# A slot of its own for each expert's first 128 pairs, listed and gathered earlier, in a two-layer mixture-of-experts kernel

## The chip, the cores and the metric

The kernel runs on one core of a Trainium2 chip. The metric is the device time of one execution, in microseconds (us). A core has a matrix engine, TensorE (PE, with its weight loads shown as PEld), and VectorE (DVE), ScalarE (ACT) and GpSimd (POOL). Each takes its instructions in the order of its own queue. SyncE (SP) only issues DMAs; ACT and POOL issue some too. The program's order of instructions on each engine is fixed when the kernel is built; at run time they wait for one another through semaphores.

## The reference

The input is 2048 tokens (8 batches of 256) of 512 numbers. Two layers follow, each a token mixing step and a mixture of eight experts of which every token uses two; each adds its result to the residual `x`:

```python
x = x + _L0_ffn_ref(_L0_cond_ref(x, ...), ...)   # paged windowed attention, then experts
x = x + _L1_ffn_ref(_L1_cond_ref(x, ...), ...)   # linear with a low-rank adapter per batch, then experts

# layer 0 experts: a common W plus a sparse change per expert
logits = jnp.clip(xt @ gate_w.T, -50.0, 50.0)
top_w, top_idx = jax.lax.top_k(logits, TOP_K)
rw = jax.nn.softmax(top_w, axis=-1)
...
# layer 1 tokens: H + (x A_b^T) B_b^T s_b, with the adapter b chosen for each batch
# layer 1 experts: top 2 of a softmax, two linear layers with biases and a gelu
h = jnp.einsum('th,ehi->eti', x, fc1_w) + fc1_b[:, None, :]
h = jax.nn.gelu(h, approximate=False)
y = jnp.einsum('eti,eih->eth', h, fc2_w) + fc2_b[:, None, :]
out = jnp.einsum('eth,te->th', y, combine)
```

## The kernel before

All is float32. Tokens are 16 tiles of 128 rows. The kernel has these stages, in program order:

1. Preparation: rotary tables, old and new keys and values, and `delta_d`, the experts' weight matrices of layer 0, made in DRAM.
2. Attention (`attend`, `gate_rows`), a loop over eight batches `b` with two tiles each. Each `attend` does four head pairs: scores `ps` (PE), mask and maximum (DVE), exponential (ACT), scaling by the sum (DVE), transposes `pp` (PE), copies `pT` (ACT) and products `po` with the values, which are copied into `oT`. `gate_rows` computes the two tiles' expert logits `lg0` with `pg` and `pt`. The PSUM pool `ps_o` has two buffers, tag "misc", for `po`, `pk`, `pq`, `pt`, `pg` and `ph`. A generator `beside` is stepped within `attend`: in the batches 6 and 7 it copies `delta_0`, half of the experts' matrices, into place (L623, ACT). `output_rows` (`ph`, L635) makes rows of `h_d`, the attention's result, for tiles 0 to 8 during the loop.
3. Middle stage of layer 0. `routing_constants`, `top2` and `normalized` choose two experts and their coefficients for all 16 tiles. `route` ranks the (token, expert) pairs of each expert and gives each pair a slot and a row. `fill_slots` turns this into lists: for each slot its 128 tokens (`token_i`) and their coefficients (`weight`), by 32 accumulated PE products `pm` of one-hot matrices `hot` (the row) and `put` (the slot). The rows 9 to 15 of `output_rows` run beside it, and the second half of the matrices, `delta_1`, is copied on POOL and ACT. Then `fold_adapters` loads layer 1's adapters and transposes and scales them (PE: `pw`, `pgb`, `pbg`).
4. The expert slots of layer 0 (`slots0`). There are 34 slots of 128 rows: a full slot belongs to one expert that is known when the program is built, a paired slot to two experts with 64 rows each, the second of which is found at run time (`owners`). `Plan` says how many of each there are: 8 full and 26 paired. A slot gathers its rows with an indirect DMA issued by POOL (`fetched`, L533, three slots ahead), turns them (`pa`, L569), multiplies by the expert's matrix (`py`, L547 full, L556 paired), scales (ACT) and adds to `sums_d` by an indirect DMA (`added`, L580). SP loads layer 1's weights `w1` and half of `w2` as soon as their memory is free. `run_rest` is a conditional part (L1752) for pairs that found no place.
5. Tokens of layer 1. The gate is folded with the adapters (`fold_gate`); the sums are read back, transposed and multiplied by the low-rank parts (`inner`), then by `wc` (`outer`). Both go over four quads of four tiles. `outer` writes `g_d` by DMAs issued from ACT. The routing of layer 1 is the same `route`, on DVE beside `outer`.
6. The expert slots of layer 1 (`slots1`): 22 full and 12 paired, gathered from `g_d`, with two matrices each (`pu` L1978, `py`), and added to `out`.

`token_i` has values up to 2175: rows from 2048 up are the filling of unused places. `h_d` and `g_d` have 128 additional rows for them, set to zero by two DMAs. The gathers of a slot in stage 4 read `h_d` as a whole, and those of stage 6 `g_d` as a whole, so each waits for every write of that tensor.

Of the kernel before, what the change touches and what calls it, by code (L numbers as in the profile page):

```python
# [19 lines left out]
P = 128  # L20
# [32 lines left out]
class Plan:  # L53
# [5 lines left out]

    PAIRED, FULL = 128 * HR, 256 * HR  # L60

    def __init__(self, full, side):
        self.full = [e for e in range(E) for _ in range(full[e])]
        self.side = [e for e in range(E) for _ in range(side[e])]
        self.F, self.D = len(self.full), len(self.side)
        self.n = self.F + self.D
        self.by_expert = []
        for e in range(E):
            t = HR * side[e]
            u = t + P * full[e]  # L70
            second = self.PAIRED + HR * (self.F + sum(side[:e]))
            whole = self.FULL + P * sum(full[:e]) - t
            first = HR * self.F - u
            self.by_expert.append((t, u, second + 1, whole - second, first - whole))


PLAN0 = Plan([1] * E, [3] * 6 + [4] * 2)
PLAN1 = Plan([3] * 6 + [2] * 2, [1] * 6 + [3] * 2)
# [3 lines left out]
def two_layer_kernel(ctx: ExitStack, tc: tile.TileContext, io: dict, out: bass.AP):  # L82
# [9 lines left out]
    h_d = dram.tile([N + P, D], F32, name="h_d")  # L92


    g_d = dram.tile([N + P, D], F32, name="g_d")
# [47 lines left out]
    def routing_constants(pool, plan=None, late=False):  # L143
# [36 lines left out]
        nc.gpsimd.iota(tok_i, pattern=[[P, NT]], base=-N, channel_multiplier=1)  # L180
# [7 lines left out]
        if plan:  # L188
            fixed_i = pool.tile([P, 5, E], I32, name="fixed_i")
# [14 lines left out]
            fixed = pool.tile([P, 5, E], F32, name="fixed")  # L204
# [5 lines left out]
    def ranks(pool, psum, consts, sel):  # L210

        earlier, ahead, same_e = consts[:3]
        flat_sel = sel.rearrange("p i e -> p (i e)")
        pst = psum.tile([P, P], F32, name="pst", tag="route_a")
        nc.tensor.transpose(pst, flat_sel, ident)
        tot = pool.tile([P, 1], F32, name="tot")
        nc.vector.tensor_reduce(tot, pst, AX.X, ALU.add)
        pn = psum.tile([P, E], F32, name="pn", tag="route_a")
        nc.tensor.matmul(pn, tot.to_broadcast([P, P]), same_e, start=True, stop=True)
        prk = psum.tile([P, NT, E], F32, name="prk", tag="route_b")  # L220
        prk2 = prk.rearrange("p i e -> p (i e)")
        nc.tensor.matmul(prk2, earlier, flat_sel, start=True, stop=False)
        nc.tensor.matmul(prk2, tot.to_broadcast([P, P]), ahead, start=False, stop=True)
# [22 lines left out]
    def two_rows(pool, rows, cf, row, coef):  # L246
# [4 lines left out]
        at = pool.tile([P, NT, E], F32, name="at")  # L251
        nc.vector.tensor_tensor(
            at, row, rows[:, 1, :, None].to_broadcast([P, NT, E]), ALU.is_equal
# [20 lines left out]
    def fill_slots(keep, pool, psum, tag, consts, slot, rem, cf, n, at_once):  # L274
# [3 lines left out]
        what = pool.tile([P, 2, NT], F32, name="what")  # L278
        nc.vector.tensor_tensor(
            what,  # L280
            tok[:, None, :].to_broadcast([P, 2, NT]),
# [5 lines left out]
        pm = psum.tile([P, 2, n], F32, name="pm", tag="route_b")  # L287
        STEP = 4
        for j in range(0, 2 * NT, STEP):
            if j % at_once == 0:  # L290
                span = slice(j, j + at_once)
                put = pool.tile([P, at_once, 2, n], F32, name="put", tag="wide")
# [18 lines left out]
            hot = pool.tile([P, STEP, P], F32, name="hot", bufs=2)  # L311
# [6 lines left out]
            for k in range(STEP):  # L318
                nc.tensor.matmul(
                    pm.rearrange("p c s -> p (c s)"),  # L320
                    hot[:, k, :],
                    put[:, (j + k) % at_once].rearrange("p c s -> p (c s)"),
                    start=(j + k == 0),
                    stop=(j + k == 2 * NT - 1),
                )
        token_i = keep.tile([P, n], I32, name=f"token_i_{tag}")
# [244 lines left out]
    def turned(pool, psum, xs):  # L571
# [3 lines left out]
        nc.vector.tensor_copy(xsT, pa)  # L575
        return xsT

    def added(sum_d, token_i, s, y):

        nc.gpsimd.indirect_dma_start(  # L580
            out=sum_d,
# [1546 lines left out]
```

## Time and profile before

| | us |
|---|---|
| median of three runs | 968.81 |
| the three runs | 976.61, 968.81, 968.16 |
| profiled execution | 970.09 |
| its span | 968.4 |
| mean granted TensorE clock, share of full speed | 0.979 |

Where the stages lie in the span of the profiled execution, by the first and last instruction of each in the trace:

| stage | from | to |
|---|---|---|
| last value product of the attention | | 397.6 |
| output rows 9 to 15 | 400.4 | 426.8 |
| list products and adapters | 426.8 | 437.6 |
| slots of layer 0 | 442.3 | 585.7 |
| tokens of layer 1 | 587.0 | 684.1 |
| slots of layer 1 | 695.3 | end |

The page counts how long each engine executed instructions; time in which it waits for a semaphore is idle. PEld runs beside PE. In a line of the timeline the first number is the start within the span, the second the duration, and in square brackets stands the idle time of that engine before it, with what released it. A row of the list of waits gives total time, number and longest of the waits of one kind. Line numbers (L533) are those of the kernel before.

### The profile page before, as it was taken

How to read it: one execution, taken by the hardware profiler on the slowest of the kernel's cores; microseconds unless marked ns; L12 is line 12 of the kernel's file. 1: busy time of each engine (PE TensorE's matmuls, PEld its weight loads, DVE VectorE, ACT ScalarE, POOL GpSimd, SP SyncE). 2: the span in 40 equal slices, each digit the busy share in tenths (PEclk: the TensorE clock that was granted, in tenths of full speed). 3: DMA queues.
4: the chain of work that ended last, by engine and by line, in shares of the span. 5: the costliest groups of instructions: out<-in, count | busy, mean ns of one | idle time of the engine just before them, and what ended most of it. 6: DMA issues, size and time to landing. Idle time of an engine off the chain costs nothing. (4 is left out here: it accounts for less than half of the span.)

```text
span 968.4 us, 14307 instructions
## 1 busy us (share of the span) xinstructions
PE 901.9 (93%) x4829; PEld 491.8 (51%) x4829; DVE 455.5 (47%) x1487; ACT 371.8 (38%) x954; POOL 360.3 (37%) x335
## 2 busy tenths in 40 slices
PE   6998889999999997897999997999599999999995
PEld 3554445655555554464433333545377777753332
DVE  5788898846857766672211112470022223223332
ACT  3676475736647599631111113401111111122221
POOL 2721656557564200405666641000233333333211
PEclk9899999999999999997999999999799999999998
DMA  6587692342432212529997768961524443443322
GB/s 194 215 307 269 225 322 45 98 114 60 138 78 61 61 44 66 189 85 326 341 255 133 129 89 222 364 230 54 185 55 76 73 69 66 77 69 63 50 27 34
DMA packets 74237, 134.62 MB, mean 139 GB/s; under 512 B 17309, under 2 KB 22941, under 8 KB 74032
## 3 DMA queue, kind: packets, MB, share of 16 engines
q0 software_dynamic: 25088, 43.68, 24.2%
q1 hardware_dynamic: 38496, 74.57, 22.1%
q10 hardware_dynamic: 10576, 15.39, 4.3%
q8 instruction: 41, 0.67, 0.3%
q14 instruction: 36, 0.29, 0.1%
HBM read 89.95 MB, written 52.56 MB: 147 GB/s over the span
## 5 line engine op out<-in xcount | busy, mean ns | idle before, releaser
L533 POOL DMA_INDIRECT xs<-g_d,token_i_l x34 | 35.2, 1035 | 230.1 <-PE pa L569 129.5
L575 DVE COPY xsT<-pa 128x512 f32<-128x512 f32 x68 | 46.8, 688 | 155.1 <-PE pa L569 146.9
L2020 DVE TENSOR_TENSOR y<-py,b 64x512 f32<-64x512 f32 (+1 forms) x46 | 31.7, 690 | 185.9 <-PE py L547 122.2
L2004 ACT ACTIVATE hs<-pu,b 128x64 f32<-128x64 f32 (+1 forms) x184 | 46.0, 347 | 186.0 <-PE pu L1978 144.5
L1451 ACT ACTIVATE s<-s,mx,roots 128x384 f32<-128x384 f32 x128 | 90.0, 706 | 14.8 <-DVE mx L1447 10.7
L556 PE MATMUL py<-delta,xsT 128*64 128x512 f32 (+1 forms) x416 | 94.8, 598 | 0.0
L1978 PE MATMUL pu<-xsT,w 128*128 128x128 f32 x704 | 83.1, 277 | 0.0
L1978 PEld LDWEIGHTS pu<-xsT,w 128*128 128x128 f32 x704 | 81.1, 194 | 0.4 <-issue 0.4
L547 PE MATMUL py<-w,hs 128*128 128x512 f32 x176 | 79.3, 593 | 0.0
L1474 PE MATMUL po<-pT,kv 128*64 128x128 f32 x768 | 69.4, 285 | 6.4 <-ACT pT L1469 6.4
L580 POOL DMA_INDIRECT out<-y,token_i_l x34 | 53.9, 1584 | 55.8 <-DVE y L2021 51.3
L1159 PE MATMUL pkv<-wkv,xb 128*128 128x512 f32 x128 | 65.4, 635 | 8.3 <-DMA wkv<-wqkvT 8.3
L1131 POOL DMA_INDIRECT delta_d<-entries,put_i x32 | 53.1, 1660 | 53.3 <-DMA delta_d<-entries,put_i 38.6
L1435 DVE CUSTOM_DVE_ANT_0 s<-ps,mask 128x384 f32<-128x384 f32 x128 | 67.2, 550 | 11.3 <-PE ps L1420 11.0
L1794 ACT ACTIVATE y<-py,weight_l 128x512 f32<-128x512 f32 x34 | 23.4, 687 | 125.7 <-PE py L556 87.0
L1474 PEld LDWEIGHTS po<-pT,kv 128*64 128x64 f32 x768 | 47.5, 137 | 43.4 <-ACT pT L1469 30.1
L580 POOL DMA_INDIRECT sums_d<-y,token_i_l x34 | 54.2, 1593 | 31.6 <-ACT y L1794 17.2
L1465 PE MATMUL pp<-ident,s 128*128 128x128 f32 x384 | 60.3, 285 | 4.3 <-DVE s L1462 3.2
L1420 PE MATMUL ps<-KT,QT 64*128 64x384 f32 x256 | 58.1, 533 | 3.5 <-DVE mx L1435 3.5
L1469 ACT COPY pT<-pp 128x384 f32<-128x384 f32 x128 | 55.8, 477 | 9.9 <-PE pp L1465 8.5
L569 PE MATMUL pa<-ident,xs 128*128 128x128 f32 x272 | 43.9, 287 | 16.8 <-DMA xs<-g_d,token_i_l 11.2
L569 PEld LDWEIGHTS pa<-ident,xs 128*128 128x128 f32 x272 | 32.7, 145 | 52.8 <-issue 46.3
(387 smaller groups left out, 1516.3 us busy)
## 6 DMA issues: line engine op xcount, KB each, us to landing
delta_d<-spread SPq DMA_DIRECT2D x16, 512.0 KB
raw<-delta_d SPq DMA_DIRECT2D x16, 512.0 KB
w<-fc_w SPq DMA_DIRECT2D x8, 1024.0 KB
w<-fc_w SPq DMA_DIRECT2D x16, 512.0 KB
part<-sums_d SPq DMA_DIRECT2D x32, 256.0 KB
xb<-xT SPq DMA_DIRECT2D x5, 1024.0 KB
sums_d<-zero SPq DMA_DIRECT2D x18, 256.0 KB
kv_new<-kvt ACTq DMA_DIRECT2D x16, 256.0 KB
```

The lines of the kernel that those rows point to most:

```text
L547: nc.tensor.matmul(py, xT[:, k, :], of_expert(experts[0])(weights(k)), start=(k == 0), stop=(k == KC - 1),)
L556: lambda k=k, h=h: nc.tensor.matmul(py[h * HR : (h + 1) * HR, :], xT[:, k, h * HR : (h + 1) * HR], of_expert(experts[h])(weights(k)), star ...
L569: nc.tensor.transpose(dst[:, k, :], src[:, k * P : (k + 1) * P], ident)
L580: nc.gpsimd.indirect_dma_start(out=sum_d, out_offset=bass.IndirectOffsetOnAxis(ap=token_i[:, s : s + 1], axis=0), in_=y, in_offset=None, b ...
L1159: nc.tensor.matmul(pkv, xb[:, k, cols], wkv[:, k, :], start=(k == 0), stop=(k == KC - 1),)
L1420: lambda r=r: nc.tensor.matmul(pss[r], QT[r * HD : (r + 1) * HD, m, t * P : (t + 1) * P], KT[r * HD : (r + 1) * HD, u, t * P : t * P + WU] ...
L1435: nc.vector.tensor_tensor_reduce(out=s, in0=pss[r], in1=mask[:, t, :], scale=1.0, scalar=NEG, op0=ALU.add, op1=ALU.max, accum_out=mx[:, r ...
L1451: nc.scalar.activation(ss[r], ss[r], AF.Exp, bias=mx[:, r : r + 1], scale=root[:, r : r + 1], accum_out=sm[:, r : r + 1],)
L1465: nc.tensor.transpose(pp[:, c * P : (c + 1) * P], s[:, c * P : (c + 1) * P], ident)
L1469: nc.scalar.copy(pT, pp)
L1474: lambda c=c, r=r: nc.tensor.matmul(po[r * HD : (r + 1) * HD, :], kvs[t + c][:, v0 + r * HD : v0 + (r + 1) * HD], pTs[r][:, c * P : (c + 1 ...
L1978: nc.tensor.matmul(pu[:, c, :], w1[:, k, plan.full[s], c * P : (c + 1) * P], xsT[:, k, :], start=(k == 0), stop=(k == KC - 1),)
```

## The change

For each layer the first eight slots now belong one to each expert, and hold that expert's first 128 pairs in token order.

- `Plan` orders the full slots so, and takes the number of tiles in which these pairs are sought: 8 for layer 0, 12 for layer 1. Layer 0 has 16 full and 18 paired slots in place of 8 and 26; layer 1 keeps its numbers. A pair of an expert's first 128 that lies in a later tile is sent to the conditional part (`far2` in `route`).
- Layer 0: the routing constants are made in batch 2 of the attention. After batch 4's `attend` for its second tile, `find_first` chooses experts for the first eight tiles, and `route_early` lists their first 128 pairs each; it is stepped within batch 5 in place of `beside`'s empty iterator. Its list products write four groups of 32 columns, summed afterwards by a transpose and a reduction; `pm` and the rank products use the "misc" buffers of `ps_o`. `slots0` is a generator now, and its first four gathers, from the first 1024 rows of `h_d`, stand on POOL, in the built order, ahead of the middle stage's work. In the middle stage `choose` handles the last eight tiles; `route` lists the other 26 slots, in two groups of 64 columns; slots 0 to 3 stand between the output rows and these list products.
- `w1` is loaded one expert per slot behind slots 8 to 15, and the first quarter of `w2` behind slots 16 to 23, each after a one-column copy on ACT; the other three quarters are loaded where the second half was.
- Adapters: the loads and the DVE and POOL part (`load_adapters`) come behind slot 6 of layer 0, the PE part (`fold_adapters`) behind the conditional part, ahead of `fold_gate`.
- Layer 1: `g_d` and the order of tiles in the routing follow the quads, and the first eight slots gather from the first 1536 rows of `g_d`, the first three quads.
- A row index for gathers (`from_i`) is kept beside `token_i`, so that `h_d` and `g_d` need no additional rows; the two DMAs that cleared them are gone. Some tables (`kcos`, `ksin`, `j_i`, `code_i`) move to another memory pool.

```diff
-        self.full = [e for e in range(E) for _ in range(full[e])]
+    def __init__(self, full, side, tiles):
+        self.full = list(range(E)) + [e for e in range(E) for _ in range(full[e] - 1)]
         self.side = [e for e in range(E) for _ in range(side[e])]
+        self.tiles = tiles
         self.F, self.D = len(self.full), len(self.side)
         self.n = self.F + self.D
         self.by_expert = []
         for e in range(E):
-            t = HR * side[e]
-            u = t + P * full[e]
-            second = self.PAIRED + HR * (self.F + sum(side[:e]))
-            whole = self.FULL + P * sum(full[:e]) - t
+            t = P + HR * side[e]
+            u = t + P * (full[e] - 1)
+            early = self.FULL + P * e
+            second = self.PAIRED + HR * (self.F + sum(side[:e])) - P
+            whole = self.FULL + P * (E + sum(full[:e]) - e) - t
             first = HR * self.F - u
-            self.by_expert.append((t, u, second + 1, whole - second, first - whole))
-PLAN0 = Plan([1] * E, [3] * 6 + [4] * 2)
-PLAN1 = Plan([3] * 6 + [2] * 2, [1] * 6 + [3] * 2)
+            self.by_expert.append((t, u, early + 1, second - early, whole - second, first - whole))
+PLAN0 = Plan([2] * E, [2] * 6 + [3] * 2, 8)
+PLAN1 = Plan([3] * 6 + [2] * 2, [1] * 6 + [3] * 2, 12)
...
+        wide = P // ways if ways > 1 else 2 * n
+        pm_tag = "misc" if hots else "route_b"
+        pm = psum.tile([P, P if ways > 1 else wide], F32, name="pm", tag=pm_tag)
...
+                put_all = pool.tile([P, at_once, wide], F32, name="put", tag="wide")
+                if wide > 2 * n:
+                    nc.gpsimd.memset(put_all, 0.0)
+                put = put_all[:, :, : 2 * n].rearrange("p a (c s) -> p a c s", c=2)
...
+            yield
+            hot = hots(j) if hots else pool.tile([P, STEP, P], F32, name="hot", bufs=2)
...
+            if ways == 1:
+                for k in range(STEP):
+                    nc.tensor.matmul(
+                        pm,
+                        hot[:, k, :],
+                        put_all[:, (j + k) % at_once, :],
+                        start=(j + k == 0),
+                        stop=(j + k == 2 * nt - 1),
+                    )
+            else:
+                in_a_row(
+                    lambda k=k: nc.tensor.matmul(
+                        pm[k % ways * wide : (k % ways + 1) * wide, :],
+                        put_all[:, (j + k) % at_once, :],
+                        hot[:, k, :],
+                        start=(j == 0 and k >= STEP - ways),
+                        stop=(j == 2 * nt - STEP and k < ways),
+                    )
+                    for k in reversed(range(STEP))
+                )
+        if ways > 1:
+            parts = pool.tile([P, P], F32, name="parts")
+            nc.scalar.copy(parts, pm)
+            pt = psum.tile([P, ways, wide], F32, name="pt", tag=pm_tag)
+            nc.tensor.transpose(pt.rearrange("p w c -> p (w c)"), parts, ident)
+            pm = pool.tile([P, wide], F32, name="sums")
+            nc.vector.tensor_reduce(pm, pt.rearrange("p w c -> p c w"), AX.X, ALU.add)
+        pm = pm[:, : 2 * n].rearrange("p (c s) -> p c s", c=2)
...
+        from_i = keep.tile([P, n], I32, name=f"from_i_{tag}")
+        if quads:
+            nc.vector.tensor_scalar(from_i, token_i, 9 * P - 1, None, ALU.bitwise_and)
+            for mask, op, by in ((6 * P, ALU.arith_shift_right, 1), (P, ALU.logical_shift_left, 2)):
+                bits = pool.tile([P, n], I32, name="bits")
+                nc.vector.tensor_scalar(bits, token_i, mask, by, ALU.bitwise_and, op)
+                nc.vector.tensor_tensor(from_i, from_i, bits, ALU.bitwise_or)
+        else:
+            nc.vector.tensor_scalar(from_i, token_i, N - 1, None, ALU.bitwise_and)
+        return from_i, token_i, weight
...
+    def route_early(keep, pool, psum, consts, sel, coef, tag, hots):
+        fixed = consts[7]
+        each = list(sel.shape)
+        nt = each[1]
+        _, prk = ranks(pool, psum, consts, sel, ("misc", "misc"))
+        row = pool.tile(each, F32, name="row")
+        nc.vector.tensor_tensor(
+            row, prk, fixed[:, 2, None, :].to_broadcast(each), ALU.add
+        )
+        mine = pool.tile(each, F32, name="mine")
+        nc.vector.scalar_tensor_tensor(mine, prk, float(P), sel, ALU.is_lt, ALU.mult)
+        nc.vector.tensor_tensor(row, row, mine, ALU.mult)
+        rows = pool.tile([P, 2, nt], F32, name="rows")
+        cf = pool.tile([P, 2, nt], F32, name="cf")
+        two_rows(pool, rows, cf, row, coef)
+        at_i = pool.tile([P, 2 * nt], I32, name="at_i")
+        nc.vector.tensor_scalar(
+            at_i, rows.rearrange("p r i -> p (r i)"), 1.0, None, ALU.subtract
+        )
+        rem_i = pool.tile([P, 2 * nt], I32, name="rem_i")
+        nc.vector.tensor_scalar(rem_i, at_i, P - 1, None, ALU.bitwise_and)
+        rem = pool.tile([P, 2 * nt], F32, name="rem")
+        nc.vector.tensor_copy(rem, rem_i)
+        nc.vector.tensor_scalar(at_i, at_i, 7, None, ALU.arith_shift_right)
+        nc.vector.tensor_scalar(at_i, at_i, 127, None, ALU.bitwise_and)
+        slot = pool.tile([P, 2 * nt], F32, name="slot")
+        nc.vector.tensor_copy(slot, at_i)
+        return (
+            yield from fill_slots(
+                keep, pool, psum, tag, consts, slot, rem, cf, E, 2 * nt, False, 4, hots
+            )
+        )
...
+        lists0 = []
+        def find_first():
+            first = slice(0, PLAN0.tiles)
+            hot = []
+            def hots(j):
+                if j % 8 == 0:
+                    hot.append(xq.tile([P, 8, P], F32, name="hot", tag="xb", bufs=3))
+                return hot[-1][:, j % 8 : j % 8 + 4, :]
+            choose(er, first)
+            found = yield from route_early(
+                dpool, er, ps_o, consts0, sel0[:, first, :], coef0[:, first, :], "e", hots
+            )
+            lists0.append((0, found))
...
+            if b == 2:
+                consts0 = routing_constants(op, PLAN0, late=True)
...
+            if b == 4:
+                beside = find_first()
+                next(beside)
...
+            def fetch(s):
+                rows_d = h_d[: plan.tiles * P, :] if plan and s < E else h_d
+                xs[s] = fetched(sx, rows_d, columns(lists, s)[0])
...
+        choose(tp, slice(PLAN0.tiles, NT))
+        SOME = 4
+        def beside_routing():
+            for i in range(EARLY + 2, NT):
+                output_rows(i, ps_y0, tp, "py")
+            for _ in range(SOME):
+                next(run0)
+        found, owner_i, left_i, places = route(
+            rp0, tp, ps_r, consts0, PLAN0, sel0, coef0, "l0", beside_routing, skip=E
+        )
+        lists0.append((E, found))
+        owner0.append(owner_i)
...
+    def load_first(e, after):
+        nc.scalar.copy(w1[:, 0, e, :1], after[:, :1])
         nc.sync.dma_start(w1[:, :, e, :], io["fc1_w"][e].rearrange("(c p) o -> p c o", p=P))
-    w2 = [wp1.tile([P, HK, E, D], F32, name="w2_0"), None]
-    def load_second(half):
-        for e in range(E):
-            nc.sync.dma_start(
-                w2[half][:, :, e, :],
-                io["fc2_w"][e].rearrange("(c p) o -> p c o", p=P)[:, half * HK : (half + 1) * HK],
-            )
-    load_second(0)
+    def load_second(part, e, after=None):
...
+    for s in range(SOME, PLAN0.n):
+        y = next(run0)
+        if s == SOME + 2:
+            consts1 = routing_constants(rdy, PLAN1, late=True, quads=True)
+            adapters = load_adapters(rp0, rp0)
+        if 0 <= s - E < E:
+            load_first(s - E, y)
+        elif 0 <= s - 2 * E < E:
+            load_second(0, s - 2 * E, y)
...
+            folding = fold_adapters(rp0, rp0, ps_g, *adapters)
...
+                at = (4 * q + j) * P
+                nc.scalar.dma_start(g_d[at : at + P, :], g)
...
+            def fetch(s):
+                rows_d = g_d[: plan.tiles * P, :] if plan and s < E else g_d
+                xs[s] = fetched(sx, rows_d, columns(lists, s)[0])
```

## The prediction

> **What bounds the kernel now.** I read the page first, then the list of waits, then the timeline around each place where TensorE (PE) stands still, and last the busy time by stage.
>
> ```profile
> span 968.4 us, 14307 instructions
> ...
> PE 901.9 (93%) x4829; PEld 491.8 (51%) x4829; DVE 455.5 (47%) x1487; ACT 371.8 (38%) x954; POOL 360.3 (37%) x335
> ...
> PE   6998889999999997897999997999599999999995
> ```
>
> PE is busy for 93% of the span. So only two things can shorten it: less PE work, or the holes in the PE row. Each digit is a slice of 24.2 us: "78" from 363 is the end of the attention, the "7" at 436 the start of layer 0's experts, the "7" at 581 the reading back of its sums, the "5" at 678 the start of layer 1's. The list of waits names the second and the last (total us, times, longest):
>
> ```profile
> POOL xs L533 <- DMA g_d<-g: 99.4, 1, 99.4
> ...
> POOL xs L533 <- DVE weight_l L329: 24.2, 1, 24.2
> ...
> PE pa L569 <- DMA xs<-g_d,token_i_l: 11.2, 1, 11.2
> ```
>
> POOL, which issues the gathers of token rows, waits for the token lists in layer 0 (`weight_l`), and for the last write of `g_d` in layer 1. The timeline of layer 0 (start, duration, operation, idle before it):
>
> ```profile
> 436.60 0.95 PE L1646 MATMUL pbg<-gw,bn 128*128 128x8 f32 x8
> 442.30 1.09 PE L569 MATMUL pa<-ident,xs 128*128 128x128 f32 x4 [4.75 <-issue]
> 444.21 1.11 PE L569 MATMUL pa<-ident,xs 128*128 128x128 f32 x4 [0.82 <-DMA xs<-h_d,token_i_l]
> 445.11 5.88 PE L547 MATMUL py<-delta,xsT 128*128 128x512 f32 x8
> ...
> 451.27 3.60 PE L547 MATMUL py<-delta,xsT 128*128 128x512 f32 x8
> ```
>
> PE stands 4.75 + 0.82 us for the first gather. Then it is slow: 5.88 us for the first product against 3.60 for the next, and 1.1 us for each of two turns (`pa`) that take 0.60 later. That is 2.28 + 2 x 0.5 = 3.3 us more. Layer 1:
>
> ```profile
> 687.65 1.09 POOL L533 DMA_INDIRECT xs<-g_d,token_i_l  x1 [99.38 <-DMA g_d<-g]
> ...
> 695.25 1.94 PE L569 MATMUL pa<-ident,xs 128*128 128x128 f32 x8 [11.21 <-DMA xs<-g_d,token_i_l]
> ...
> 697.22 4.60 PE L1978 MATMUL pu<-xsT,w 128*128 128x128 f32 x32
> ```
>
> Here the hole is 11.21 us, and the slow start after it costs 1.5 us (1.94 for eight turns against 1.2, 4.60 for `pu` against 3.78 in later slots).
>
> **The change part by part.** All sums are in us against the profiled execution: span 968.4, its own time 970.09, which lies 1.28 above the median of 968.81. I subtract from the median at the end.
>
> *Layer 0, middle stage.* The first eight slots now need only tiles 0 to 7, whose lists exist before the attention ends. In the new order of instructions their first gathers stand right behind the last `po` product, and PE runs the output rows (24 us: seven times 3.43), then slots 0 to 3, before it needs the second set of lists. So the hole (5.6) and its slow start (3.3) go: -8.9. The first idle stretch of this stage, 2.1 us from 397.6 to 399.7 or so, stays at most partly: -1 (0 to -2). What is late next is the gather of slot 8: between its list products and its use stand slots 5 to 7 and part of the list work, 8.4 us by the steady slot time, against the 6.4 us from 435.89 (`token_i`) to 442.30 before. That is thin; I put 2 (0 to 5) against it and against the first turns waiting for POOL. POOL gets four gathers (1.0 us each) ahead of four copies of `delta_1`, which ended at 417.55 and were first used at 445; now they are used from about 427. Moving them later by 5 leaves 4 us; if that cover went, each us would be a us of PE.
>
> *Plan of layer 0.* Eight of 26 paired slots become full ones. A full slot takes PE 3.87 (the period of the lines above), a paired one 4.17 in steady state: 8 x 0.30 = -2.4. Expert counts worked out from the reference's inputs fill every early slot (168 to 300 pairs in the first 1024 tokens, at least 128 needed), and 17 of 18 paired units are used, so nothing spills into the conditional part.
>
> *Adapters.* Their PE work (transposes 0.53 + 0.28 + 0.60, `pgb` 2 x 1.07, `pbg` 0.95: 4.2 us with its seams) leaves the middle stage: -4.2. It goes behind the branch after layer 0's slots, where PE is idle anyway:
>
> ```profile
> 580.00:590.00 10.00, 8.62 (x45) 4.03 (x42) 0.00 (x0) 2.86 (x6) 3.77 (x3) 1.00 0.57 64
> 590.00:600.00 10.00, 7.03 (x25) 2.59 (x23) 3.46 (x5) 2.25 (x4) 0.00 (x0) 0.83 0.89 270
> 600.00:610.00 10.00, 8.71 (x79) 5.08 (x82) 5.97 (x14) 4.27 (x8) 0.00 (x0) 1.00 1.05 381
> ```
>
> (Columns: window, length, then busy us of PE, weight loads, DVE, ACT, POOL; granted clock; DMA share; GB/s.) The idle time is 1.38 + 2.97 + 1.29 = 5.6 us, and until 603 PE waits for the sums' reads, which the fold does not touch. The chain of copies between its products (0.58 each on ACT) can still hold up the gate. +2 (0 to +5).
>
> *Loads.* The eight 1 MB loads of `w1` move from one burst (343 to 364 GB/s from 437 on, no PE wait beside it) to one per slot behind slots 8 to 15, and a quarter of `w2` behind slots 16 to 23, each behind a one-column ACT copy. Late `w2_1` grows from 4 to 6 MB: at 345 GB/s that is 6 us more, from a landing at 650 to 656, while the first use is near 688. ACT has over 2 us free per slot. Zero; if the cover were gone, a late weight costs its own lateness once.
>
> *Layer 1.* Early slots now gather from the first three quads of `g_d`. In the built program the first gather waits for the writes up to the third quad, and of PE only for a product of the second, so it can start near 672 (third quad's last product at 670.05, its copy and write behind it). The old chain from gather issue to `pa` took 695.25 - 687.65 = 7.6, which ends near 680, before PE leaves the last quad at 684.05. The hole and its slow start go: -12.7; five small DVE operations on the list, beside products, and a little left at the seam: +0.7. Gelu's table load (1.28, ACT) now lies beside PE work.
>
> *Attention.* This part pays. Sixteen list products in groups of 32 columns, the rank products and one transpose add some 2.75 us of PE (from `pm` at 1.90 for 16 and the turns above), and choosing, ranks, lists and constants add about 16 us of DVE, 13 of them in batch 5 (hot 0.69 each, choosing half of what ran at 400.9 to 409.5, the rest small ones of 0.1 to 0.3). The rows of batches 5 and 6:
>
> ```profile
> 306.75:342.30 35.55, 35.13 (x230) 19.95 (x231) 24.24 (x87) 22.18 (x60) 11.30 (x9) 1.00 0.26 75
> 342.30:370.40 28.10, 25.43 (x208) 15.90 (x208) 17.89 (x73) 26.63 (x57) 0.00 (x0) 1.00 0.19 57
> ```
>
> 24.2 + 13 = 37 us of DVE into 38 of PE: DVE is full, and softmax operations queue behind list operations. Besides, the lists' sum `pm` holds one of the two PSUM buffers for nine tiles of `po` and `pk`, each of which must then wait for the one before to be copied out (0.27 on ACT with 0.1 to 0.2 before and after, partly beside 0.43 of `pp`). Lower bound 2.75 (all waits beside other work; a gain is excluded, since work is only added); upper bound 2.75 + 9 x 1.0 for the buffer + some 5 of DVE overhang = 17. No row shows one buffer alone; I take 7, nearer the low end, since PE already waits only 0.2 to 0.9 for such copies.
>
> [...] During `delta` copies on POOL a small DVE operation takes seven times its usual time, but beside a POOL gather it does not:
>
> ```profile
> 308.96 1.09 POOL L1060 DMA_INDIRECT kv<-cache,idx_old  x1 [0.30 <-PE ps L1420]
> ...
> 309.60 0.15 DVE L1459 RECIPROCAL sm<-sm 128x2 f32<-128x2 f32 x1
> ...
> 401.83 5.21 POOL L623 COPY delta<-raw 128x1024 f32<-128x1024 f32 x2 [1.47 <-DMA raw<-delta_d]
> ...
> 405.07 2.07 DVE L483 TENSOR_SCALAR sel_l<-sel_l 128x128 f32<-128x128 f32 x1
> ```
>
> [...] By the rows only copies block, and POOL's copies do not run in batch 5: 0. [...]
>
> **Sum.** -8.9 - 1 + 2 - 2.4 - 4.2 + 2 - 12.7 + 0.7 + 7 = -17.5: 968.8 - 17.5 = 951.3.
>
> **Rivals.** (a) One of the two early gathers is late after all. In layer 1 a DMA write lands 3 us after its product and the gather queues behind `w2_1`'s 6 MB; half to all of the 12.7 stays: 958 to 964. For: POOL's wait there was for DMA, and the loads end near 656 only by estimate. Against: 12 us of cover. (b) The attention pays the upper bound and batch 6, which ACT already fills (26.63 of 28.10), does not take it back: +17 to +25, 961 to 969, no change. For: the two rows above. Against: PE at 35.13 of 35.55 with DVE at 68% shows slack between engines. (c) Slower: the spread loads collide with the gathers in slots 8 to 23. A gather is issued three slots (12 us) ahead and took some 5 us; 1 MB ahead of it in the same engines is 3.0 us at 345 GB/s. If the load delayed each gather past its lead by 3.0 us, 16 x 3.0 = 48: 999. It decides from 17.5 / 16 = 1.1 us a slot (no gain), 1.7 (slower). Against: the burst of 12 MB before delayed one turn by 0.82 and no other. (d) It does not do what it says: lists spill and the conditional part runs, one slot of 4.2 and a routing of about 25 us, 980. The counts speak against it.
>
> **How the numbers follow.** Forecast as summed 0.62 (942 to 959, nearly all faster), (a) 0.13 (two thirds no change), (b) 0.15 (a fifth slower, a fifth faster), (c) 0.06, (d) 0.04. One per cent, 9.7 us, is about what a measurement of this kernel can tell from no change: under 959.1 is faster, over 978.5 slower. Faster 0.68, within 0.20, slower 0.12. The best corner (attention 2.75, no stalls, fold free) is 941; leaving out the upper part of (b), (c) and (d) the range ends at 967.
>
> **What would show it.** Right: no PE hole over 2 us between the output rows and slot 0's product, the first `py` at 3.60; slots 8 to 15 at 3.87; under 2 us before the first `pa` of layer 1, with `xs<-g_d` issued before the last quad ends; batch 5 some 7 us longer than 35.55. Wrong: batch 5 longer by over 15, a turn that waits in slot 8, fetches waiting on `g_d`'s last writes, or the fold adding its 4.2 before 603.

## The result and the profile after

The changed kernel takes 959.09 us (median of 7 runs, 957.88 to 964.74) against 969.36 for the kernel before (7 runs). The ratio is 0.987, with a 95% interval from 0.983 to 0.990. The forecast was 951.3, with a range from 941 to 967: right in direction and within its range, but the gain is 10 us by the medians, 13 by the ratio, in place of 17.5.

The page of the kernel after, first its span, busy times and slices:

```profile
span 959.2 us, 14359 instructions
...
PE 901.9 (94%) x4804; PEld 494.0 (52%) x4804; DVE 465.2 (49%) x1558; ACT 374.7 (39%) x971; POOL 362.8 (38%) x339
...
PE   6999989997999998798899998999999999999995
```

PE is busy for 901.9 us in both kernels, so the difference of the spans is idle time. (Busy time includes what a slow clock adds, so it isn't the same as work: the eight products `py` behind slot 8's turn below keep PE busy for 5.29 us, at a granted clock of 0.69 from the turn on, where eight such products take 3.60 at 1.00.) The "7" and "5" at the start of the two expert stages are gone. A new "7" stands at slice 9 (the first is 0), from 216 to 240 us, in the middle of the attention.

The timeline says where the time went. The table is put together from it, for this kernel, the one before and the variants of the next section; each column is the distance of two events in that kernel's profiled execution. "Attention" is from batch 0's `pg` to the last `po`, "batch 2" the distance of two `pg` within it; "middle and slots" ends with the first product behind the conditional part, "fold" with the first `px`, "outer" with the last `pc`, "hole" with layer 1's first `pu`. What is missing to the span is the time ahead of `pg`.

| kernel | attention | batch 2 | middle and slots | fold | outer | hole | layer 1 slots | span |
|---|---|---|---|---|---|---|---|---|
| before | 243.7 | 39.3 | 189.4 | 16.0 | 81.0 | 13.2 | 271.2 | 968.4 |
| after | 254.6 | 48.0 | 177.6 | 19.6 | 81.9 | 1.3 | 270.6 | 959.2 |
| e1_count | 246.9 | 39.2 | 177.3 | 17.8 | 80.2 | 1.3 | 270.0 | 946.0 |
| e2_turns | 253.8 | 47.2 | 174.1 | 17.2 | 80.2 | 1.3 | 270.7 | 951.5 |
| e3_some3 | 254.7 | 47.2 | 173.1 | 20.9 | 81.0 | 1.3 | 270.2 | 955.5 |
| e4_wn | 254.5 | 48.1 | 177.8 | 16.4 | 80.2 | 1.3 | 270.3 | 955.1 |
| u1_g_whole | 254.8 | 48.3 | 178.2 | 20.2 | 80.8 | 12.6 | 271.9 | 971.6 |
| u2_h_whole | 255.3 | 48.6 | 183.6 | 20.9 | 80.9 | 1.3 | 270.4 | 963.7 |
| u3_plan | 246.9 | 40.3 | 180.1 | 19.8 | 80.2 | 1.3 | 270.5 | 953.2 |
| u4_fold | 254.9 | 48.3 | 179.3 | 17.5 | 82.8 | 1.3 | 270.8 | 958.0 |
| e123 | 247.2 | 39.2 | 169.9 | 21.6 | 80.7 | 1.3 | 270.9 | 945.3 |
| e1234 | 247.2 | 39.2 | 169.2 | 16.4 | 80.2 | 1.3 | 270.7 | 939.0 |

From before to after: attention +10.9, middle and slots -11.8, fold +3.6, outer +0.9, hole -11.9, slots of layer 1 -0.6, ahead of `pg` -0.3: -9.2, the difference of the spans. Stages that an edit leaves alone still differ by 1 to 2.6 us from kernel to kernel: the slots of layer 1 (270.0 to 270.9 without u1_g_whole), batch 2 where its hole is in place (47.2 to 48.6; u3_plan apart), outer (80.2 to 82.8). The fold varies more (16.4 to 21.6), and why is told with e4_wn. Of each variant one execution was profiled. The changed kernel was not run again beside the variants; the kernel before was, and its median lay between 969.36 and 970.60.

Layer 1 went as intended. The timeline of the kernel after at its start:

```profile
676.13 1.09 POOL L656 DMA_INDIRECT xs<-g_d,from_i_l  x1 [88.95 <-issue]
...
687.22 1.04 PE L692 MATMUL pa<-ident,xs 128*128 128x128 f32 x8
688.65 3.81 PE L2160 MATMUL pu<-xsT,w 128*128 128x128 f32 x32 [0.39 <-issue]
```

The first gather is issued 11 us before PE leaves the last quad, `pa` follows without a wait, and eight turns take 1.04 where they took 1.94 in the kernel before (granted clock 0.73 from 695.25 to 702).

The start of layer 0's slots:

```profile
434.70 1.04 PE L692 MATMUL pa<-ident,xs 128*128 128x128 f32 x8
438.91 0.66 PE L366 MATMUL pm<-hot,put 128*64 128x128 f32 x8 [3.17 <-DVE put L341]
439.51 3.69 PE L670 MATMUL py<-delta,xsT 128*128 128x512 f32 x8
...
473.63 0.63 PE L692 MATMUL pa<-ident,xs 128*128 128x128 f32 x4 [2.42 <-DMA xs<-h_d,from_i_l]
474.09 5.29 PE L670 MATMUL py<-delta,xsT 128*128 128x512 f32 x8
```

The 4.75 us hole with its slow start is gone, but two smaller holes stand in its place: 3.17 us at the first product of the second lists, which the built order put ahead of slot 0, and 2.42 us at slot 8's turn, the first of the second lists. The second has a slow start of its own: the `py` behind it takes 5.29 us where such a product takes 3.60.

The new hole of the attention lies in batch 2, not in batch 5. These are lines of PE, DVE and POOL of the same stretch, ordered by engine:

```profile
223.53 1.12 PE L1524 MATMUL pk<-ident,kv 128*128 128x128 f32 x4 [6.52 <-DVE KT L1527]
...
222.38 0.23 DVE L184 CAST count<-count_i 128x128 f32<-128x128 int32 x1 [7.57 <-POOL count_i L182]
...
222.80 0.68 DVE L1527 COPY KT<-pk 128x512 f32<-128x512 f32 x1
...
212.63 1.56 POOL L1264 DMA_INDIRECT delta_d<-entries,put_i  x1 [3.40 <-DMA delta_d<-entries,put_i]
217.27 1.55 POOL L1264 DMA_INDIRECT delta_d<-entries,put_i  x1 [3.08 <-DMA delta_d<-entries,put_i]
218.29 3.85 POOL L1244 TENSOR_TENSOR roots<-rs,minus_half 128x8 f32<-128x8 f32 x2
221.54 0.80 POOL L182 IOTA count_i<- 128x128 int32 x1
```

Read from the end: POOL makes `count_i` only at 221.54, behind two additions to `delta_d` (each of which waits 3 us for the one before) and two `roots`. DVE's cast of it is pinned in program order, so DVE stands 7.57 us with nothing else allowed past it. The copy of `KT`, which PE needs, is four instructions behind the cast, so PE stands 6.52. The `pk` after it takes 1.12 us, where the same four transposes took 0.66 at 214.71.

### The profile page after: what moved, and what is told of

It is laid out like the page before. It is cut to its first block, busy times and chain, and to the rows that moved or that the text cites. A ratio compares the mean times of both kernels' runs of the same rounds, so it can differ in the third digit from the quotient of the medians.

```text
span 959.2 us, 14359 instructions
## 1 busy us (share of the span) xinstructions
PE 901.9 (94%) x4804; PEld 494.0 (52%) x4804; DVE 465.2 (49%) x1558; ACT 374.7 (39%) x971; POOL 362.8 (38%) x339
## 5 line engine op out<-in xcount | busy, mean ns | idle before, releaser
L656 POOL DMA_INDIRECT xs<-g_d,from_i_l x34 | 36.5, 1074 | 223.5 <-PE pa L692 133.4
L1585 ACT ACTIVATE s<-s,mx,roots 128x384 f32<-128x384 f32 x128 | 90.0, 707 | 13.2 <-DVE mx L1581 10.9
L679 PE MATMUL py<-delta,xsT 128*64 128x512 f32 (+1 forms) x288 | 65.5, 598 | 0.0
L1603 ACT COPY pT<-pp 128x384 f32<-128x384 f32 x128 | 55.9, 477 | 17.7 <-PE pp L1599 17.2
L1554 PE MATMUL ps<-KT,QT 64*128 64x384 f32 x256 | 60.1, 552 | 2.6 <-DVE mx L1569 2.6
L670 PE MATMUL py<-delta,xsT 128*128 128x512 f32 x128 | 60.2, 611 | 0.0
L2065 PE MATMUL pc<-wc,x1T 128*128 128x512 f32 x128 | 60.0, 609 | 0.0
L1231 PE MATMUL pq<-wq,xb 128*128 128x512 f32 x128 | 58.1, 598 | 0.4 <-DVE KT L1527 0.4
L768 PE MATMUL ph<-woT,oT 128*128 128x512 f32 x128 | 56.8, 594 | 0.0
## 6 DMA issues: line engine op xcount, KB each, us to landing
w<-fc_w SPq DMA_DIRECT2D x8, 768.0 KB, 11.8
```

What stands on the lines that cost most here:

```text
L670: nc.tensor.matmul(py, xT[:, k, :], of_expert(experts[0])(weights(k)), start=(k == 0), stop=(k == KC - 1),)
L679: lambda k=k, h=h: nc.tensor.matmul(py[h * HR : (h + 1) * HR, :], xT[:, k, h * HR : (h + 1) * HR], of_expert(experts[h])(weights(k)), star ...
L768: nc.tensor.matmul(ph, oTs[i // 2][:, k, (i % 2) * P : (i % 2 + 1) * P], woT[:, k, :], start=(k == 0), stop=(k == KC - 1),)
L1231: nc.tensor.matmul(pq, xcols[:, k, :], wq[:, k, :], start=(k == 0), stop=(k == KC - 1))
L1554: lambda r=r: nc.tensor.matmul(pss[r], QT[r * HD : (r + 1) * HD, m, t * P : (t + 1) * P], KT[r * HD : (r + 1) * HD, u, t * P : t * P + WU] ...
L1585: nc.scalar.activation(ss[r], ss[r], AF.Exp, bias=mx[:, r : r + 1], scale=root[:, r : r + 1], accum_out=sm[:, r : r + 1],)
```

## The experiments

**e1_count: is it this one iota?** `count_i` used the buffer of `low_i`, which DVE reads at about 212 us; so POOL could not make it before that, and in the built order the additions and roots stood in front of it. The edit frees the buffer:

```diff
-        low_i = pool.tile([P, NT * E], I32, name="low_i")
-        after(nc.vector.tensor_scalar(low_i, dif_i, E - 1, None, ALU.bitwise_and))
         dif = pool.tile([P, NT * E], F32, name="dif", tag="row")
         after(nc.vector.tensor_copy(dif, dif_i))
+        after(nc.vector.tensor_scalar(dif_i, dif_i, E - 1, None, ALU.bitwise_and))
...
-        after(nc.vector.tensor_copy(ahead, low_i))
+        after(nc.vector.tensor_copy(ahead, dif_i))
...
-        count_i = pool.tile([P, P], I32, name="count_i", tag="low_i")
+        count_i = pool.tile([P, P], I32, name="count_i")
```

> The changed kernel with one edit: the iota count_i no longer shares its buffer with low_i (low_i is made in place in dif_i), so that POOL can make it early. Theory A (in batch 2 DVE's casts of the routing constants, pinned in order, stand behind this one iota, which waits for low_i's reader and then behind two delta_d adds and two roots operations on POOL: 7.57 us of DVE, 6.52 of PE and a cold clock after it): batch 2 falls from 48.0 to about 39.4 us, no DVE wait on POOL above 1 us there, total 8 to 9 us below the changed kernel, about 950.5 (ratio to the kernel before about 0.980). Rival B (batch 2 is longer because DVE's constants or POOL's queue as a whole are in the way): the wait moves to another constant or to the roots, batch 2 stays above 44, total above 955.

Measured: 951.35 us (ratio to before 0.981, 0.975 to 0.986). Batch 2 is 39.2 in place of 48.0. Its windows (columns as in the prediction), the kernel after first, then e1_count:

```profile
220.00:230.00 10.00, 6.47 (x32) 4.19 (x33) 5.57 (x23) 3.31 (x10) 4.50 (x5) 0.66 0.08 26
```

```profile
220.00:230.10 10.10, 9.92 (x84) 6.04 (x84) 9.97 (x42) 8.80 (x26) 6.28 (x5) 1.00 0.14 28
```

PE is full again and its clock at 1.00, with the same constants on DVE and POOL's additions as late as before (217.26 for the roots against 218.29). POOL now makes `count_i` at 6.14 us. So it is the wait on this one operation, not the constants' work. Theory A stands.

**u1_g_whole: does the split of `g_d` fill layer 1's hole?**

```diff
-                rows_d = g_d[: plan.tiles * P, :] if plan and s < E else g_d
+                rows_d = g_d
```

> The changed kernel, but the first eight slots of layer 1 gather from the whole of g_d, so they wait for the last quad's writes. Theory A (the split of g_d is what removed the hole before layer 1's slots): a hole of about 11 us with a cold clock after it comes back, total about 11.5 above the changed kernel, 970 to 971. Rival B (the hole went because of the other order of stores or loads, w2 above all): a hole under 6 us, total under 965.

Measured: 971.5 us, ratio to before 1.000 (0.998 to 1.003). The hole is back as it was:

```profile
697.81 1.94 PE L692 MATMUL pa<-ident,xs 128*128 128x128 f32 x8 [10.66 <-DMA xs<-g_d,from_i_l]
```

12.4 us above the changed kernel: this one line is worth more than the whole gain. Theory A stands.

**u2_h_whole: the same for `h_d`.**

```diff
-                rows_d = h_d[: plan.tiles * P, :] if plan and s < E else h_d
+                rows_d = h_d
```

> The changed kernel, but the first eight slots of layer 0 gather from the whole of h_d, so they wait for the last output rows (tile 15). Theory A (it takes both the early lists and the split of h_d to fill the hole before slot 0): PE stands for some 7 to 9 us behind the output rows (copy, write, 1 us of gather descriptors, landing, turn) at a cold clock, total 8 to 11 above the changed kernel, 967 to 970. Rival B (early lists alone are enough, since the old hole was the lists' 5 us chain): a hole under 4 us, total under 963.

Measured: 964.62 us, +5.5 on the changed kernel, less than A said and more than B. The hole is there:

```profile
445.71 1.09 PE L692 MATMUL pa<-ident,xs 128*128 128x128 f32 x4 [4.56 <-issue]
447.16 1.12 PE L692 MATMUL pa<-ident,xs 128*128 128x128 f32 x4 [0.35 <-DMA xs<-h_d,from_i_e]
```

The hole and its cold start are much like those of the kernel before (4.75 and 0.82). Middle and slots grew by 6.0, but that is not the price of this hole alone, since three other waits changed with it. DVE has `put` ready before PE wants it, so the 3.17 us at the first `pm` are gone; the list products come earlier against the slots, so slot 8's 2.42 us and the slow start behind them are gone too. Against that stands a new wait of 3.56 us ahead of it, at `pn` (0.33 in the kernel after). The first gathers, which now wait for the rows, no longer stand ahead of POOL's copies of `delta_1`; these start 8.0 us behind the last `po` in place of 9.8, and fall on DVE's choice of experts (POOL, DVE, PE):

```profile
417.44 2.02 POOL L748 COPY delta<-raw 128x1024 f32<-128x1024 f32 x1 [0.59 <-DMA raw<-delta_d]
417.74 1.80 DVE L618 TENSOR_TENSOR coef<-coef,sm 128x64 f32<-128x64 f32 x1
419.80 0.39 PE L237 MATMUL pn<-same_e,tot 128*128 128x8 f32 x2 [3.56 <-DVE tot L233]
```

The same `coef` takes 0.22 in the kernel after. So the hole in front of slot 0 is shown to come from the whole `h_d`, and the early lists alone do not fill it; what the split is worth by itself is not separated.

**e2_turns: why does PE wait for `put`?** In the kernel after, the turns of slots 0 and 1 come behind the output rows, and their copies stand on DVE behind the three `put` operations:

```profile
435.58 1.06 DVE L329 TENSOR_TENSOR put<-from_slot,count 128x832 f32<-128x832 f32 x1
...
436.68 1.03 DVE L335 TENSOR_TENSOR put<-put,cf 128x832 f32<-128x832 f32 x1
437.74 1.03 DVE L341 TENSOR_TENSOR put<-put,what 128x832 f32<-128x832 f32 x1
438.68 1.28 DVE L698 COPY xsT<-pa 128x512 f32<-128x512 f32 x2
```

Their rows had been fetched long before (gathers issued at 409 to 413). The edit calls the turns earlier; the built order then also puts `pm` behind slot 3:

```diff
             xT = {s: turn(s) for s in range(s0, min(s0 + 2, end))}
+            if plan:
+                yield xT
...
+        next(run0)
         choose(tp, slice(PLAN0.tiles, NT))
```

> The changed kernel with the turns (pa, xsT) of slots 0 and 1 called ahead of the second choice of experts, in place of behind the output rows. Theory A (the 3.17 us hole at the first list product is a queue on DVE: xsT of slots 0 and 1 stands behind the three put operations): the hole goes, slot 0's product follows the output rows directly, total 3 us below the changed kernel, about 956; the second hole of 2.42 before slot 2's to slot 8's turns may grow by up to 1. Rival B (PE would wait for put or for delta_1 anyway): a wait of 2 to 4 us appears at slot 0's product or at the next list product, total unchanged near 959.

Measured: 955.13 us. Middle and slots fell by 3.5, and of the waits only slot 8's is left:

```profile
469.87 0.63 PE L692 MATMUL pa<-ident,xs 128*128 128x128 f32 x4 [2.35 <-DMA xs<-h_d,from_i_l]
```

Theory A stands. (Its span is lower by 7.7; 3.5 of that is the edit's stage. The fold was 2.4 shorter in this execution, with the same instructions.)

**e3_some3: slot 8's gather.** In the kernel after, the lists' last steps and the gather run so (DVE reduces the products' sum and makes the row indices, POOL fetches, PE turns):

```profile
463.50 0.29 DVE L381 TENSOR_REDUCE sums<-pt 128x64 f32<-128x128 f32 x1 [2.54 <-PE pt L379]
...
464.66 0.32 DVE L397 TENSOR_SCALAR from_i_l<-token_i_l 128x26 int32<-128x26 int32 x1
...
466.73 1.10 POOL L656 DMA_INDIRECT xs<-h_d,from_i_l  x1 [0.56 <-issue]
```

From 463.50 to the turn at 473.63 are 10.1 us, with 6.9 from issue to turn where the first gather before had 5.3. Slot 8's turn stands ahead of slot 7's product, so only the products of slots 5 and 6 lie beside this chain; they end at 471.2 and do not cover it. The edit is `SOME = 3` in place of 4.

> The changed kernel with three slots instead of four ahead of the second list's products (SOME = 3), so slot 8's gather can start one slot (3.9 us) earlier. Theory A (the 2.42 us hole at 473.63 is the chain list products, transpose, reduction, token, gather, and nothing else): the hole goes, total 2 to 2.5 below the changed kernel, about 957. Rival B (POOL's queue of adds and constants decides when that gather is issued): the hole shrinks by under 1 us. DVE's list operations could also come too late for the earlier products: then PE waits up to 3 us there instead.

Measured: 955.57 us; the wait at slot 8 is gone, the one at the first `pm` is 2.62, and middle and slots fell by 4.5. That is more than expected, because the slow start behind the hole goes as well. The product behind slot 8's turn:

```profile
471.76 3.60 PE L670 MATMUL py<-delta,xsT 128*128 128x512 f32 x8
```

2.42 for the hole, 5.29 - 3.60 = 1.69 for the slow start and 0.55 for the shorter wait at `pm` make 4.66. Theory A had the hole right and left out its slow start.

**u3_plan: full against paired slots.** `PLAN0 = Plan([1] * E, [3] * 6 + [4] * 2, 8)`.

> The changed kernel with 8 full and 26 paired slots in layer 0, as before, in place of 16 and 18. By the steady periods (3.87 full, 4.17 paired) the total rises by 8 x 0.30 = 2.4 us, to about 961.5. If paired slots cost nothing more beside the loads of w1, no change (under 1 us); if the loads or PE's register reads hit paired slots there, over 4 us.

Measured: 956.57 us, 2.5 below the changed kernel where a rise of 2.4 was expected. The table tells why: middle and slots rose by 2.5, just as the periods say, but batch 2 took 40.3 in place of 48.0. The instructions around `count_i` stand in the same order as in the kernel after; POOL's chain of additions merely ran some 5 us ahead, and the cast waits little:

```profile
216.97 0.23 DVE L184 CAST count<-count_i 128x128 f32<-128x128 int32 x1 [1.38 <-POOL count_i L182]
```

So the wait of batch 2 is a race between POOL's chain and DVE, and the total alone would have misled here. Why the chain is ahead in this kernel was not tried, and only one of its four runs (954.86 to 958.60) was profiled.

**u4_fold: the fold back in the middle stage.** `folding = fold_adapters(rp0, rp0, ps_y0, *load_adapters(rp0, rp0))` behind the call of `route`, in the buffers of tag "py".

> The changed kernel with the adapters' loads and fold back in the middle stage (behind slot 3, beside the second lists' products). Forecast's theory A (most of the fold is hidden in the idle PE time behind the conditional part): total rises by 2 to 4 us. Rival B (the fold costs as much behind the conditional part as in the middle, since it delays the gate's chain: the trace shows 19.6 us to the first px in place of 16.0): total within 1 us of the changed kernel, with 3 to 4 us less from the conditional part to the first px. It can also shorten the wait of slot 8, as the fold is PE work beside the gather.

Measured: 960.56 us, 1.5 above, with four runs from 955.03 to 961.67, so a change of the total is not shown. Middle and slots rose by only 1.7: the fold's 4.2 us fill slot 8's wait, and its slow start goes, while the wait at the first `pm` is 3.87 with a slow start there. The way to `px` fell by 2.1, not by 3 to 4. Neither theory fits as stated. As the kernel was made, moving the fold brought next to nothing, as B says; but e4_wn shows that B's reason is wrong, since with one copy moved the stage takes 16.4 with the fold in it, against 16.0 before the change without it.

**e4_wn: why is the fold's stage longer?** One of four copies `wn` went to DVE and stood there behind additions that wait for the sums' reads (DVE, then PE, kernel after):

```profile
597.73 0.69 DVE L2020 TENSOR_TENSOR part<-part,part 128x512 f32<-128x512 f32 x1 [0.64 <-DMA part<-sums_d]
598.34 0.68 DVE L130 COPY wn<-pw 128x512 f32<-128x512 f32 x1
...
599.08 1.05 PE L131 MATMUL acc<-wn,gw 128*32 128x512 f32 x4 [3.28 <-DVE wn L130]
```

The transposes it copies had ended at 595.4. The edit, in `fold_gate`'s call of `seen_through`:

```diff
-            nc.any.tensor_copy,
+            nc.scalar.copy,
```

> The changed kernel with all four copies wn of the gate's folding on ACT (one of them had been given to DVE, where it stands behind additions of part that wait for the sums' reads). Theory A (the longer way from the conditional part to the first px, 19.6 us in place of 16.0, is mostly that copy: PE stands 3.28 us for it, and the clock falls after it): the hole before the last acc falls below 1.5 us, px comes 2 to 4 us earlier, total 956 to 957. Rival B (px waits for the sums' reads in any case, as they are paced by DMA): px no more than 1 us earlier, total unchanged.

Measured: 955.57 us. The wait at `acc` is gone and the way to `px` is 16.4, 0.4 more than before the change, with the fold's 4.2 us in it:

```profile
598.04 1.04 PE L131 MATMUL acc<-wn,gw 128*32 128x512 f32 x2
599.76 0.66 PE L138 MATMUL pt<-ident,parts 128*128 128x128 f32 x4 [0.68 <-ACT parts L135]
```

Theory A stands. It also goes with the stage's variation: where the copy stands on DVE, the wait at `acc` goes from 2.13 us (e2_turns, stage 17.2) to 3.94 (e123, stage 21.6), and in some of these kernels the products behind it start slowly (four `acc` in 1.92 in place of 1.05).

**e123 and e1234: together.**

> The three edits together (count_i in a buffer of its own, early turns of slots 0 and 1, three slots ahead of the second lists). If the three waits are independent, their savings add: 8.5 + 3 + 2.3, so 13 to 14 below the changed kernel, about 945, ratio near 0.974. Rival: with the first hole gone PE reaches the second lists' products 3.2 us earlier and, with three slots, another 3.9 earlier, so DVE's put and hot operations come last and a wait of 2 to 4 us appears there: about 948.

> All four edits together. If A holds for the last edit: 2 to 4 us below the three edits together (944.3), about 941, ratio to the kernel before 0.970. Under B unchanged at 944.

Measured: 944.26 us (ratio 0.973, 0.967 to 0.979) and 940.89 us (ratio 0.969, 0.966 to 0.972). The savings add: attention -7.4, middle and slots -7.7 with three edits (3.5 and 4.5 alone); the fourth takes the fold from 21.6 to 16.4. No wait for `put` appeared. e1234 beats both kernels: 29 us below before, 18 below the change as it was made.

## Why the forecast came out as it did

- *The hole of layer 1* (-12.7 + 0.7): right, -11.9 in the hole, -0.6 behind it; shown by u1_g_whole.
- *Layer 0, hole and slow start* (-8.9): the mechanism was right; the hole comes back without the split (u2_h_whole). But against the reserve of 2 us for waits, two came, 3.17 and 2.42 with 1.69 of slow start: 7.3. I had named the second, slot 8's gather, and mis-sized it: from `token_i` to the turn it took 9.8 us (463.83 to 473.63), not 6.4, and PE had 7.4 of work in front of it, not 8.4. The first I had not named: what I priced was DVE's work, hidden by the output rows, and not its queue, where two small copies that PE needs stood behind the lists. Middle and slots still gave -11.8 in place of -14.5, and part of that is luck: the list products take 3.1 us less of PE in the new form, a gain that I had left out, and the idle time at the stage's start fell by 2.6 in place of 1. Some 2 us of this sum I can't place. The list products before and after:

```profile
L319 PE MATMUL pm<-put,hot 128*128 128x68 f32 x64 | 7.7, 271 | 0.0
```

```profile
L366 PE MATMUL pm<-hot,put 128*64 128x128 f32 x64 | 4.6, 280 | 3.2 <-DVE put L341 3.2
```

- *Plan* (-2.4): right, +2.5 in its stage when undone (u3_plan), where the two waits of layer 0 differ by no more than 0.4.
- *Adapters* (-4.2, +2): mis-sized. The way to `px` grew by 3.6, because the later chain put a copy on a queue paced by DMA (e4_wn). The idle 5.6 us was there and took up the fold, but PE then waits 3.28 us for that copy, which the +2 was too small for; without the wait the way to `px` grows by 0.4.
- *Attention* (+7): the total was +10.9, and the reason was wrong. I put all of it in batch 5, on a full DVE and one PSUM buffer less. Batch 5 took +2.8, which is the 2.75 of PE work that I gave as the lower bound; batch 4, where the choice is made, +1.0; batch 6 gave 1.2 back. The windows of the kernel after show PE at 37.88 of 38.30 there, with DVE at 30.62 (+6.4, not +13):

```profile
315.80:354.10 38.30, 37.88 (x262) 20.98 (x261) 30.62 (x113) 21.49 (x59) 11.18 (x9) 1.00 0.25 70
```

  What I had left at nothing, the constants in batch 2, cost +8.7: I had counted 3 us of DVE work for them, and no wait. The step that failed is that I asked how long the added operations last, and not which queue each of them must first wait in.
- *POOL's work beside DVE* (0): right for batch 5, where POOL ran gathers, `roots` and an addition to `delta_d`, but no copy; the list operations there cost PE nothing beyond its own work. In the middle stage, beside POOL's copies of some 2.04 us and also beside one fill (MEMSET, 1.80 us), some operations that otherwise take 0.2 to 0.3 us took 1.3 to 2.05, together some 8 us of DVE ahead of `put` by an estimate from their durations; others beside the same copies kept their time (`row_l` 0.29 at 418.59). Two of the long ones, with what POOL ran beside each (kernel after; in the kernel before each takes 0.17, `owner_i_l` with 26 columns):

```profile
421.67 1.93 DVE L443 SCALAR_TENSOR_TENSOR boff<-boff,fixed 128x8 f32<-128x8 f32 x1
...
424.35 1.77 DVE L293 TENSOR_SCALAR owner_i_l<-owner 128x18 int32<-128x18 f32 x1
...
421.54 2.03 POOL L748 COPY delta<-raw 128x1024 f32<-128x1024 f32 x1 [1.45 <-DMA raw<-delta_d]
424.29 1.80 POOL L327 MEMSET put<- 128x2048 f32 x1 [0.72 <-DVE owner L292]
```

  What part of the 3.17 us that is was not tried; e2_turns removes the wait with the copies left as they are.
- *The rivals.* Neither (a), (c) nor (d) happened: no gather of layer 1 was late, no slot from 9 on waited with the loads spread, and the conditional part did not run. (b) came nearest in size, by another way.
- *The signs named in advance* are mixed. Layer 1 and slots 8 to 15 came as said. But a hole of over 2 us did stand between the output rows and slot 0's product, a turn did wait in slot 8, which was named as a sign of being wrong, and batch 5 grew by 2.8 and not 7. The misses of the parts mostly have one sign: 2.7 in middle and slots, 1.6 in the fold, 0.9 in outer and 3.9 in the attention, against 0.5 more gained in layer 1 and 0.3 ahead of `pg`.

## What to carry to other kernels

When work is moved into a stage that seems to have room, list for each moved instruction what it waits for and what stands behind it on its engine: here two turns' copies, one copy of `wn` and one cast, each under 1 us, cost 3.2, 3.3 and 8.7 us, and mending their places (4.0, 3.5 and 7.7 us by the medians of e2_turns, e4_wn and e1_count) brought more than the whole change had. A buffer shared through a tag is a hidden wait: the second user can't be made before the first one's reader is done, however early it is written in the program (`count_i` was made at 221.54 us in `low_i`'s buffer, at 6.14 in one of its own). And read a changed kernel by stage, not by total: u3_plan was 2.5 us faster while the part that it changes was 2.5 us slower.

## What the runs showed of the hardware that was not expected

How long PE stands does not by itself decide whether it starts slowly afterwards. At the first product `py` after the wait for `put`, it looks like a sharp limit: a wait of 2.62, 2.87 or 3.17 us (e3_some3, e1_count, the kernel after) leaves `py` at 3.69 us, while 3.28, 3.57 or 3.87 us (e4_wn, u3_plan, and both u1_g_whole and u4_fold) makes it 5.38. The lines of e4_wn:

```profile
439.96 0.66 PE L366 MATMUL pm<-hot,put 128*64 128x128 f32 x8 [3.28 <-DVE put L341]
440.56 5.38 PE L670 MATMUL py<-delta,xsT 128*128 128x512 f32 x8
```

But at slot 8's turn, 35 us later, the limit doesn't hold. Waits of 2.35, 2.41 and 2.42 us (e2_turns, e1_count, the kernel after) make the next `py` 5.29 or 5.30, while 2.20, 2.37 and 2.38 us (u3_plan, e4_wn, u1_g_whole) leave it at 3.60. The granted clock, the third number from the end of a row, tells the two apart; the kernel after, then e4_wn, from the turn to the end of that `py`:

```profile
473.63:479.20 5.57, 5.57 (x12) 2.51 (x13) 2.52 (x10) 0.00 (x0) 4.54 (x4) 0.69 0.78 168
```

```profile
476.32:480.20 3.88, 3.88 (x12) 1.95 (x13) 2.46 (x9) 0.00 (x0) 2.96 (x4) 1.00 0.77 168
```

At both places the slow start costs the same 1.69 us: 5.38 - 3.69 and 5.29 - 3.60. In the kernels that have both waits, the slow start came at exactly one of the two places: at slot 8 in the kernel after and e1_count, at `put` in e4_wn, u1_g_whole and u3_plan. What decides between them was not tried.
